# A gated attention and mixture-of-experts layer: twenty held tiles in place of twelve, a shorter gate chain and rows normalized by ScalarE

## The chip, the cores and the metric

The kernel runs on one core of a Trainium2 chip, in float32 throughout. Its time is the device time of one execution in microseconds. "Before" is the median of three runs; the profile is of one further execution.

Engines: PE is TensorE (matrix multiply), DVE is VectorE, ACT is ScalarE, POOL is GpSimd, SP is SyncE, which issues most DMAs. In the trace each engine starts its instructions in the order in which the program puts them, so an instruction that waits holds up all behind it on its engine.

## The reference

Input is `x`, 8 sequences of 512 tokens with 1024 features, and a context of the same shape. Cut to what matters:

```
x = x + tanh(g_xattn) * mlstm(layernorm(x), ctx, ctx, Wi, bi, Wf, bf, ln_scale)
x = x + tanh(g_ffn)   * moe(layernorm(x), router, gate, up, down, shared_gate, shared_up, shared_down)

mlstm(q, k, v):                       # 16 heads of 64
    ig, fg = [q k v] @ Wi + bi, [q k v] @ Wf + bf
    log_f  = log_sigmoid(fg);  cum = cumsum(log_f)
    log_D  = cum[s] - cum[t] + ig[t]  for t <= s, else -inf
    m      = max over t of log_D;  D = exp(log_D - m)
    C      = (q k^T / 8) * D
    h      = (C / (max(|sum C|, exp(-m)) + 1e-6)) @ v
    return per-head layernorm(h) * ln_scale

moe(y):                               # 4096 tokens, 16 experts of width 512, top 2
    shared = (silu(y @ shared_gate) * (y @ shared_up)) @ shared_down      # width 1024, every token
    routed = sum over the two best experts of weight * expert(y)
    return shared + routed
```

## The kernel before

The 4096 tokens are 32 tiles of 128 rows (`NT`), four to a sequence. The work has two stages.

**The attention loop** (`for i in range(1, NT)`, L856) takes one tile per turn and is pipelined by hand: in turn `i` the queries, keys and gates of tile `i + 1` are prepared while tile `i` gets its scores and values, and tile `i - 1` is finished: normalized per head, added to `x`, normalized (`finish_rows`), written out as `y`, transposed (`turn_rows`) and routed (`route_products`, `finish_route`, then `route_group` and `place_group` once per four tiles).

The steps of one tile that the prediction follows are these. `prep_gates` multiplies the partial sums by `sums` into `pg` (L464, one per tile, pinned behind the second half of the scores of the tile before). The 16x128 gate rows then pass between DVE and ACT: `f` (L471, bias L473), `z = min(-f, f)` (L477), its exponential, `u = 1 + z`, its logarithm, a correction of that logarithm (L481 to L489: it multiplies `ln(u)` by `z / (u - 1)`, with a guard for `u = 1`), then two scans, and `nm`, the negated running maximum (L501). `nm` is written to DRAM (L505) and read back broadcast over 128 partitions into `d` (L506). `prep_columns` (L530 and after) transposes the rows into `cols`, and POOL cuts the upper triangle off `d` (L535). `prep_weights` exponentiates `d` on ACT, one head after the other (L577), `scores` multiplies it by the products of queries and keys (L586 on PE, L593 on DVE) in two halves of eight heads; both halves use the two PSUM banks with tag `a`, so the second waits for the DVE product of the first. After the second half comes the next tile's `pg`.

**The shared expert in the loop.** For all tiles but the last 12 (4 x `HELD`), the shared expert is cut into units of work for TensorE: per pair of tiles eight chunks (`chunk`, L248: gate and up for 128 hidden columns, then Silu on ACT and a product on DVE) and four half projections (`project_down`, L265). They lie in a queue, `units`; `fill(share)`, called four times per turn, takes as many as `share` has added up to. The first four turns have a share of 0.75, the later ones of

```
each = (6 * (NT - 4 * HELD) - 1 - 3 * FIRST - RESERVE) / (4 * (NT - 1 - FIRST))
```

which is 99/108 = 0.917 with `HELD = 3`. Eight units (`RESERVE`) are left for the end of the loop. `behind` holds the last instruction of the last unit run, and `pinned` puts an instruction behind it in its engine's order. The chunks' weights are streamed from DRAM again for each pair.

**The experts and the held tiles** (`for e in range(JOBS)`, `JOBS = NE + 2 * HELD`): sixteen jobs for the routed experts, then two jobs per four held tiles, for which half the shared expert's hidden columns are one more "expert" over 512 tokens. All use a seven-product scheme in place of eight block products (`Step`, `down_tiles`), whose sums of blocks DVE and POOL make.

A scheduler orders each engine's instructions from the program's order, dependencies and priorities, so units stand interleaved with the loop's steps. Loads of `x` and `kv` (`load_x`, `load_kv`) and all traffic of the loop go through SP's queue; at the start some loads go through ACT's queue. `row_stats` (L124, L126) makes mean and variance on DVE, `inverse_deviation` the reciprocal deviation on POOL (L114, L117), and `normed` the normalized row on DVE (L426), twice per tile.

Of the kernel before, what the change touches and what calls it, by code (L numbers as in the profile page):

```python
# [18 lines left out]
P = 128  # L19
S = 512  # L20
D = 1024
# [14 lines left out]
HELD = 3  # L36
# [6 lines left out]
def flamingo_layer(  # L43
# [50 lines left out]
    nc.scalar.dma_start(gates_t[:, 0:1], g_xattn.unsqueeze(0).to_broadcast([P, 1]))  # L94
    nc.scalar.dma_start(gates_t[:, 1:2], g_ffn.unsqueeze(0).to_broadcast([P, 1]))
# [210 lines left out]
    with ExitStack() as actx:  # L306
# [50 lines left out]
        nc.scalar.dma_start(lnsc, ln_scale.unsqueeze(0).to_broadcast([P, D]))  # L357
# [21 lines left out]
        nc.scalar.dma_start(acc_d[T : T + P, :], zeros[:, :D])  # L379
# [44 lines left out]
        def normed(row, mean, rstd):  # L424
            o = wk.tile([P, D], F32, tag="row", name="row", bufs=2)
            normed.last = nc.vector.tensor_scalar(o, row, mean, rstd, ALU.subtract, ALU.mult).ins  # L426
            return o

        def prep_norm(i: int):
            q = toks[i]  # L430
            mv = row_stats(sm, q.x)
            rstd = inverse_deviation(sm, mv[:, 1:2], LN_EPS, [P, 1])
            q.xn = normed(q.x, mv[:, 0:1], rstd)
# [25 lines left out]
        def prep_gates(i: int, after=()):  # L459
# [16 lines left out]
            z, u, lnu, eq = (row(n, 1) for n in ("z", "u", "lnu", "eq"))  # L476
# [4 lines left out]
            nc.vector.tensor_scalar(u, u, -1.0, None, ALU.add)  # L481
# [997 lines left out]
```

## Time and profile before

| | |
|---|---|
| runs before | 3212.82 us median of 3 (3210.32 to 3215.99) |
| the profiled execution | 3221.06 us |
| its span, first to last instruction | 3219.3 us |
| mean granted TensorE clock | 0.975 |
| attention loop, to the experts' first product | 1453.1 us |
| experts' jobs, 1453.1 to 2752.4 us | TensorE busy 1296.9 of 1299.3 us |
| the rest of the held jobs, 2752.4 to 3219.3 us | TensorE busy 455.6 of 466.9 us |

TensorE's busy time is a union of modelled matmul spans, so it says where TensorE had work, not that it ran at its peak. A row of a stretch gives its start and end, its length, the busy time of PE, PE's weight loads, DVE, ACT and POOL with the number of instructions, then the granted clock, the share of the DMA engines' time and the GB/s. A row of the timeline gives start, length, engine, line, operation, the tile written and those read, and the shapes; in square brackets the idle time ahead of it and what ended it. TensorE issues each float32 matmul as two instructions, so a half projection of eight matmuls shows as x16.

### The profile page before, as it was taken

How to read it: one execution, taken by the hardware profiler on the slowest of the kernel's cores; microseconds unless marked ns; L12 is line 12 of the kernel's file. 1: busy time of each engine (PE TensorE's matmuls, PEld its weight loads, DVE VectorE, ACT ScalarE, POOL GpSimd, SP SyncE). 2: the span in 40 equal slices, each digit the busy share in tenths (PEclk: the TensorE clock that was granted, in tenths of full speed). 3: DMA queues.
4: the chain of work that ended last, by engine and by line, in shares of the span. 5: the costliest groups of instructions: out<-in, count | busy, mean ns of one | idle time of the engine just before them, and what ended most of it. 6: DMA issues, size and time to landing. Idle time of an engine off the chain costs nothing.

```text
span 3219.3 us, 42324 instructions
## 1 busy us (share of the span) xinstructions
PE 3107.8 (97%) x16127; PEld 2294.8 (71%) x16127; DVE 1798.4 (56%) x3573; ACT 863.7 (27%) x1825; POOL 1295.2 (40%) x993
## 2 busy tenths in 40 slices
PE   6999989999999999999999999999999999999999
PEld 5778777786877867666666666666677777776666
DVE  5655666767667675644444444444454445455554
ACT  3444444443544544311111111111111111100000
POOL 2213232323231323235555555555565544444342
PEclk7889999999999999999999999999999999999999
DMA  6766565666656666553544545444454544645330
GB/s 191 206 210 190 174 181 171 191 187 187 197 170 191 184 188 174 161 198 130 141 121 115 141 134 136 122 119 128 129 142 135 141 129 131 187 163 173 106 130 27
DMA packets 371280, 501.52 MB, mean 156 GB/s; under 512 B 24352, under 2 KB 262480, under 8 KB 366944
## 3 DMA queue, kind: packets, MB, share of 16 engines
q1 hardware_dynamic: 342560, 425.00, 42.1%
q0 software_dynamic: 24752, 72.44, 10.8%
q8 instruction: 130, 2.13, 0.3%
q10 hardware_dynamic: 3760, 1.31, 0.2%
q14 instruction: 78, 0.64, 0.1%
HBM read 394.57 MB, written 114.61 MB: 158 GB/s over the span
## 4 chain that ended last, share of the span: by engine, by line
PE 51%; DVE 3%; issue 0%; DVEq 0%
PE pq L1281 48%; PE ptx L1199 2%; PE pq L1382 1%; DVE hsum L1345 1%; DVE hsum L1346 1%; DVE hT L1303 1%; DVE up L1302 0%; DVE tsum L1230 0%; DVE tsum L1228 0%; DVE tsum L1227 0%; DVE yo L1356 0%; DVE hT L1347 0%; DVE u L1363 0%; DVE u L1362 0%; DVE xT L1202 0%
## 5 line engine op out<-in xcount | busy, mean ns | idle before, releaser
L1281 PE MATMUL pq<-xT,w 128*128 128x256 f32 (+1 forms) x2112 | 513.4, 393 | 8.5 <-DVEq L1262 8.5
L1281 PEld LDWEIGHTS pq<-xT,w 128*128 128x128 f32 x2112 | 401.7, 191 | 101.3 <-issue 13.4
L1281 PE MATMUL pq<-tsum,wsum 128*128 128x256 f32 (+1 forms) x1408 | 349.8, 391 | 0.0
L248 PE MATMUL pgu<-sh_yT,swg 128*128 128x256 f32 (+1 forms) x1280 | 299.2, 384 | 1.3 <-DMA swg<-L_ffn_shared_gate_w_dram 1.3
L1281 PEld LDWEIGHTS pq<-tsum,wsum 128*128 128x128 f32 x1408 | 264.0, 190 | 49.5
L265 PE MATMUL pso<-sh_down,sh_hT 128*128 128x512 f32 x640 | 286.8, 599 | 2.3 <-DVE sh_hT L254 2.3
L248 PE MATMUL pgu<-sh_yT,swu 128*128 128x256 f32 (+1 forms) x1280 | 278.1, 371 | 0.9 <-DMA swu<-n_L_ffn_shared_up_w_dram 0.9
L248 PEld LDWEIGHTS pgu<-sh_yT,swu 128*128 128x128 f32 x1280 | 235.3, 191 | 31.5 <-DMA swu<-n_L_ffn_shared_up_w_dram 1.1
L1305 DVE TENSOR_TENSOR hT<-pq,u 128x256 f32<-128x256 f32 (+1 forms) x176 | 77.2, 439 | 322.4 <-PE pq L1281 318.8
L248 PEld LDWEIGHTS pgu<-sh_yT,swg 128*128 128x128 f32 x1280 | 233.1, 197 | 33.5 <-issue 3.2
L114 POOL TENSOR_SCALAR ve<-bmv 128x1 f32<-128x1 f32 x64 | 15.6, 243 | 580.7 <-DVE bmv L126 578.5
L1246 POOL TENSOR_TENSOR wsum<-w 128x512 f32<-128x512 f32 x88 | 113.6, 1290 | 295.1 <-PE pq L1281 290.8
L265 PEld LDWEIGHTS pso<-sh_down,sh_hT 128*128 128x128 f32 x640 | 119.0, 192 | 136.8 <-issue 132.1
L1302 DVE TENSOR_TENSOR up<-pq,u 128x256 f32<-128x256 f32 (+1 forms) x176 | 77.1, 438 | 223.7 <-PE pq L1281 222.3
L1012 POOL DMA_INDIRECT acc_d<-yo,row_i x64 | 102.1, 1595 | 184.4 <-ACT yo L1374 70.4
L1281 PE MATMUL pq<-wd,hT 128*128 128x512 f32 x352 | 169.6, 597 | 6.9 <-DVE hT L1303 5.4
L1281 PE MATMUL pq<-xT,wsum 128*128 128x256 f32 (+1 forms) x704 | 174.9, 391 | 0.0
L1281 PE MATMUL pq<-tsum,w 128*128 128x256 f32 (+1 forms) x704 | 174.9, 391 | 0.0
L1306 ACT ACTIVATE hT<-hT 128x256 f32<-128x256 f32 (+1 forms) x176 | 75.4, 429 | 339.2 <-DVE hT L1305 339.2
L1281 PE MATMUL pq<-dsum,hT 128*128 128x512 f32 x352 | 165.4, 592 | 0.0
L1281 PE MATMUL pq<-dsum,hsum 128*128 128x512 f32 x352 | 165.4, 592 | 0.0
L1356 DVE TENSOR_TENSOR yo<-pq,u 128x512 f32<-128x512 f32 x176 | 118.9, 686 | 76.9 <-PE pq L1281 56.5
(265 smaller groups left out, 5478.4 us busy)
## 6 DMA issues: line engine op xcount, KB each, us to landing
swg<-L_ffn_shared_gate_w_dram SPq DMA_DIRECT2D x88, 512.0 KB, 5.0
swu<-n_L_ffn_shared_up_w_dram SPq DMA_DIRECT2D x88, 512.0 KB, 5.8
w<-in_L_ffn_gate_w_dram SPq DMA_DIRECT2D x16, 2048.0 KB, 9.8
w<-in_L_ffn_up_w_dram SPq DMA_DIRECT2D x16, 2048.0 KB, 9.9
wd<-in_L_ffn_down_w_dram SPq DMA_DIRECT2D x16, 2048.0 KB, 8.0
d<-nm_d SPq DMA_DIRECT2D x31, 1024.0 KB, 6.2
x_sb<-in_x_dram SPq DMA_DIRECT2D x32, 512.0 KB, 4.9
kv<-in_ctx_dram SPq DMA_DIRECT2D x32, 512.0 KB, 6.0
```

Source lines behind the costliest of these rows:

```text
L248: last = nc.tensor.matmul(pg[:, half, :n], lhsT=w[:, c, :], rhs=st["yT"][:, c, :n], start=(c == 0), stop=(c == NC - 1),)
L265: last = nc.tensor.matmul(po, lhsT=st["hT"][:, k, t * P : (t + 1) * P], rhs=sh_down[:, k, cols], start=(k == 0), stop=(k == 2 * NFC - 1),)
L1012: nc.gpsimd.indirect_dma_start(out=rows, out_offset=bass.IndirectOffsetOnAxis(ap=index, axis=0), in_=row, in_offset=None, compute_op=ALU.add,)
L1199: nc.tensor.transpose(pt[:, c, :], row[:, (half * 4 + c) * P : (half * 4 + c + 1) * P], ident)
L1246: nc.gpsimd.tensor_tensor(s1, a21, a22, ALU.add)
L1281: nc.tensor.matmul(out, lhsT=left[:, c, :], rhs=right[:, c, :], start=(c == 0), stop=(c == chunks - 1))
L1302: nc.vector.tensor_tensor(up, part, other, ALU.add)
L1303: nc.vector.tensor_tensor(out, out, up, ALU.mult)
L1305: nc.vector.tensor_tensor(out, part, other, ALU.add)
L1306: nc.scalar.activation(out, out, AF.Silu)
L1345: nc.vector.tensor_tensor(s1, a21, a22, ALU.add)
L1356: nc.vector.tensor_tensor(rows[t][:, halves[half]], part, other, ALU.add)
```

## The change

`HELD` goes from 3 to 5: the last 20 tiles are held, 12 have units in the loop, there are 26 jobs in place of 22, and `each` becomes 51/108 = 0.472. The other edits: rows are normalized by ACT with a scale and a bias per partition (the bias made by POOL); the gates' logarithm is corrected by subtracting the rounding error `(u - 1) - z` without the division, and `bias_f` is added in ACT's copy; `y` is turned, and its routing products made, one unit and half the values later; the two pinned instructions of routing and columns are now pinned behind the last unit; `kv` has three buffers and is loaded along with `x`; the loads of ACT's queue move to POOL's and, for `wf`, to SP's; and at the start the second tile's norm follows the first tile's gates.

```diff
-HELD = 3
+HELD = 5
...
-    nc.scalar.dma_start(gates_t[:, 0:1], g_xattn.unsqueeze(0).to_broadcast([P, 1]))
-    nc.scalar.dma_start(gates_t[:, 1:2], g_ffn.unsqueeze(0).to_broadcast([P, 1]))
+    nc.gpsimd.dma_start(gates_t[:, 0:1], g_xattn.unsqueeze(0).to_broadcast([P, 1]))
+    nc.gpsimd.dma_start(gates_t[:, 1:2], g_ffn.unsqueeze(0).to_broadcast([P, 1]))
...
-            nc.vector.bn_stats(st[:, k, :], row[:, k * 512 : (k + 1) * 512])
+            row_stats.last = nc.vector.bn_stats(st[:, k, :], row[:, k * 512 : (k + 1) * 512]).ins
...
-            q.kv = wk.tile([P, D], F32, tag="kv", name="kv")
+            q.kv = wk.tile([P, D], F32, tag="kv", name="kv", bufs=3)
...
-        nc.scalar.dma_start(w3[:, :, NH:], wf.rearrange("(c p) h -> p c h", p=P))
+        nc.sync.dma_start(w3[:, :, NH:], wf.rearrange("(c p) h -> p c h", p=P))
...
-        nc.scalar.dma_start(bias_i, bi.unsqueeze(1))
-        nc.scalar.dma_start(bias_f, bf.unsqueeze(1))
+        nc.gpsimd.dma_start(bias_i, bi.unsqueeze(1))
+        nc.gpsimd.dma_start(bias_f, bf.unsqueeze(1))
...
-        nc.scalar.dma_start(lnsc, ln_scale.unsqueeze(0).to_broadcast([P, D]))
+        nc.gpsimd.dma_start(lnsc, ln_scale.unsqueeze(0).to_broadcast([P, D]))
...
-        nc.scalar.dma_start(acc_d[T : T + P, :], zeros[:, :D])
+        nc.gpsimd.dma_start(acc_d[T : T + P, :], zeros[:, :D])
...
-            nc.scalar.dma_start(rw, router_w)
+            nc.gpsimd.dma_start(rw, router_w)
...
-        def normed(row, mean, rstd):
+        def normed(row, mv):
+
+            rstd = inverse_deviation(sm, mv[:, 1:2], LN_EPS, [P, 1])
+            shift = sm.tile([P, 1], F32, tag="shift", name="shift")
+            nc.gpsimd.tensor_scalar(shift, mv[:, 0:1], rstd, -1.0, ALU.mult, ALU.mult)
             o = wk.tile([P, D], F32, tag="row", name="row", bufs=2)
-            normed.last = nc.vector.tensor_scalar(o, row, mean, rstd, ALU.subtract, ALU.mult).ins
+            nc.scalar.activation(o, row, AF.Identity, scale=rstd, bias=shift)
             return o
...
-            nc.scalar.copy(f, pg[32:48, :])
+            nc.scalar.activation(f, pg[32:48, :], AF.Identity, bias=bias_f)
             nc.vector.tensor_scalar(a, pg[0:NH, :], bias_i, None, ALU.add)
-            nc.vector.tensor_scalar(f, f, bias_f, None, ALU.add)
...
             nc.scalar.activation(lnu, u, AF.Ln)
-            nc.vector.tensor_scalar(u, u, -1.0, None, ALU.add)
-            nc.vector.tensor_scalar(eq, u, 0.0, None, ALU.is_equal)
-            nc.vector.tensor_add(u, u, eq)
-            nc.vector.reciprocal(u, u)
-            nc.vector.tensor_mul(u, u, z)
-            nc.vector.tensor_mul(lnu, lnu, u)
-            nc.vector.tensor_mul(eq, eq, z)
-            nc.vector.tensor_add(lnu, lnu, eq)
-            nc.vector.scalar_tensor_tensor(f, f, 0.0, lnu, ALU.min, ALU.subtract)
+            nc.vector.scalar_tensor_tensor(u, u, -1.0, z, ALU.add, ALU.subtract)
+            nc.vector.scalar_tensor_tensor(f, f, 0.0, u, ALU.min, ALU.add)
+            nc.vector.tensor_sub(f, f, lnu)
...
-        def prep_columns(i: int):
+        def prep_columns(i: int, after=()):
             q, last, first = toks[i], i % NS == NS - 1, i % NS == 0
             pc = ps.tile([P, 5, NH], F32, tag="tr", name="pc")
-            nc.tensor.transpose(pc.rearrange("p k h -> p (k h)"), rows3[i % 2], ident[:80, :80])
+            with ExitStack() as order:
+                pinned(order, after)
+                nc.tensor.transpose(pc.rearrange("p k h -> p (k h)"), rows3[i % 2], ident[:80, :80])
...
-        with tc.issue_after(normed.last):
+        with tc.issue_after(row_stats.last):
             prep_gate_weights()
             prep_values(0)
         gate_products(0)
         prep_gates(0)
         prep_columns(0)
-        with tc.issue_after(normed.last):
+        with tc.issue_after(toks[0].gated):
             prep_norm(1)
-        with tc.issue_after(normed.last):
             prep_router()
...
             if i + 2 < NT:
                 load_x(i + 2)
+                load_kv(i + 2)
             fill(share)
             values(i, 0)
             values(i, 1)
             if nxt:
                 prep_values(i + 1)
+            fill(share)
             if back:
                 turn_rows(i - 1)
-            fill(share)
-            if back:
-                route_products(i - 1)
             values(i, 2)
             valued = values(i, 3)
-            if back:
-                whole = finish_route(i - 1, valued)
             head_scale(i)
             if not last:
                 grow(i)
-            if i + 2 < NT:
-                load_kv(i + 2)
+            if back:
+                with tc.issue_after(valued[0]):
+                    route_products(i - 1)
+            fill(share)
+            if back:
+                whole = finish_route(i - 1, behind)
             if nxt:
-                prep_columns(i + 1)
-            fill(share)
+                prep_columns(i + 1, behind)
```

`prep_norm` and `finish_rows` now pass the statistics to `normed`, which calls `inverse_deviation` itself; `toks[i].gated` is the instruction that makes `nm`.

More of the change, by code (lines that the diff above doesn't have):

```diff
@@ L430, in prep_norm @@
             q = toks[i]
-            mv = row_stats(sm, q.x)
-            rstd = inverse_deviation(sm, mv[:, 1:2], LN_EPS, [P, 1])
-            q.xn = normed(q.x, mv[:, 0:1], rstd)
+            q.xn = normed(q.x, row_stats(sm, q.x))
         def prep_values(i: int):
@@ L470, in prep_gates @@
             a, en, w = (rows3[i % 2][32 * k : 32 * k + NH, :] for k in range(3))
-            nc.scalar.copy(f, pg[32:48, :])
+            nc.scalar.activation(f, pg[32:48, :], AF.Identity, bias=bias_f)
             nc.vector.tensor_scalar(a, pg[0:NH, :], bias_i, None, ALU.add)
-            nc.vector.tensor_scalar(f, f, bias_f, None, ALU.add)
-            z, u, lnu, eq = (row(n, 1) for n in ("z", "u", "lnu", "eq"))
+            z, u, lnu = (row(n, 1) for n in ("z", "u", "lnu"))
             nc.vector.scalar_tensor_tensor(z, f, -1.0, f, ALU.mult, ALU.min)
@@ L500, in prep_gates @@
             nm = row("nm", 1)
-            nc.vector.tensor_scalar(nm, q.m, -1.0, None, ALU.mult)
+            q.gated = nc.vector.tensor_scalar(nm, q.m, -1.0, None, ALU.mult).ins
             q.d = wk.tile([P, NH, P], F32, tag="d", name="d")
@@ L679, in finish_rows @@
             nc.sync.dma_start(x1_d[i] if i < NT - 4 * HELD else acc_d[i * P : (i + 1) * P, :], q.x)
-            mv = row_stats(sm, q.x)
-            rstd = inverse_deviation(sm, mv[:, 1:2], LN_EPS, [P, 1])
-            q.y = normed(q.x, mv[:, 0:1], rstd)
+            q.y = normed(q.x, row_stats(sm, q.x))
             nc.sync.dma_start(y_d[i * P : (i + 1) * P, :], q.y)
@@ L845, in flamingo_layer @@
         load_x(2)
+        load_kv(2)
         prep_columns(1)
-        load_kv(2)
         route_products(0)
```

## The prediction
> **What bounds the kernel now.** I read the busy table first, then the slices, then stretches of the two stages, then single instructions. The busy table and the TensorE slices:
>
> ```profile
> PE 3107.8 (97%) x16127; PEld 2294.8 (71%) x16127; DVE 1798.4 (56%) x3573; ACT 863.7 (27%) x1825; POOL 1295.2 (40%) x993
> PE   6999989999999999999999999999999999999999
> ```
>
> The reader is to see one bound, TensorE, in nearly every slice. But it is made of two stages. Up to about 1453 us the attention loop runs, with the shared expert's matmuls strewn between its steps; after that the experts and the held tiles run. `pg` (L464) comes once a tile, so its times cut the loop into tiles: 219.5 us is tile 5's, 1313.4 us tile 31's, 26 tiles in 1093.9 us, 42.07 us each. The stretch, and inside it one single tile (569.0 to 604.9), by busy time:
>
> ```profile
> core 0: us, PE busy (x) PEld busy (x) DVE busy (x) ACT busy (x) POOL busy (x), PEclk, DMA share, GB/s
> 219.50:1313.40 1093.90, 1048.62 (x7198) 816.12 (x7196) 741.85 (x1637) 494.73 (x1104) 298.61 (x258) 0.96 0.62 183
> 569.00:604.90 35.90, 34.25 (x278) 29.45 (x277) 27.33 (x65) 21.19 (x45) 8.15 (x7) 1.00 0.70 203
> ```
>
> Per tile TensorE is busy 40.33 of 42.07 us, DVE 28.5, ACT 19.0, POOL 11.5. What a unit of shared-expert work costs is read off TensorE's timeline: a half projection (L265) from its start to the next instruction, and a chunk (L248, gate and up):
>
> ```profile
> 605.21 7.13 PE L265 MATMUL pso<-sh_down,sh_hT 128*128 128x512 f32 x16
> 612.18 0.39 PE L608 MATMUL pav<-state,eb 128*128 128x130 f32 x2
> ...
> 647.92 3.72 PE L248 MATMUL pgu<-sh_yT,swg 128*128 128x256 f32 x16
> 654.93 0.39 PE L608 MATMUL pav<-state,eb 128*128 128x130 f32 x2
> ```
>
> That is 6.97 and 7.01 us, 6.99 on the mean. A held job, in the chain of waits (start, length), has a fixed period at the end of the kernel:
>
> ```profile
> 2825.98 66.64 PE pq L1281 x262
> 2899.52 66.64 PE pq L1281 x262
> ```
>
> 2899.52 - 2825.98 = 73.54 us a job, with DVE's sums between the two included.
>
> **The change, part by part.** *Eight tiles more are held.* A pair of tiles costs 8 chunks and 4 half projections in the loop, so four pairs take 48 units out: 48 x 6.99 = 335.5 us. By the formula for `each` a tile's share falls from 4 x 0.917 to 4 x 0.472 units, 1.78 fewer, over the 27 tiles from 5 on: 12.43 us each. Added are two quartets of two jobs: 4 x 73.54 = 294.2 us, sure, since that stage has no idle TensorE to take them. If the loop shrinks by exactly the TensorE time removed, a tile takes 42.07 - 12.43 = 29.64 us, and the kernel changes by 294.2 - 335.5 = -41.3 us. All else is whether the loop can do 29.64. The break-even is 42.07 - 294.2/27 = 31.17 us a tile: a margin of 1.5 us.
>
> *DVE.* In the stretch L426 takes 42.3 us, now gone to ACT; the bias and nine instructions of the correction, ten groups (L473, L481 to L489) of 6.9, 5.7, 5.7, 7.2, 24.3, 6.9, 7.9, 6.3, 7.1 and 7.1 us, go, 85.1; three new ones of the same 16x128 kind come at about 7.1 each, 21.3. Fewer evictions: 1.78 units at (8 x 0.41 + 4 x 0.74)/12 = 0.52 us (rows L254, L270) are 0.93 a tile. So 28.5 - 1.63 - 2.45 - 0.93 = 23.5 us a tile, 79% of 29.64: not the bound, but fuller than its 68% now.
>
> *ACT.* Two 128x1024 rows a tile with scale and bias. No such row exists; ACT's 128x512 copy takes 0.587 us and its 128x256 row 0.39, so between 0.59 + 2 x 0.197 = 0.98 and twice 0.587 = 1.17; I take 1.1, since the growing part dominates: 2.2 a tile. The Silu evictions fall by 1.19 x 0.384 = 0.46. So 19.0 + 2.2 - 0.5 = 20.7 us, 70%, at nothing while the loop is TensorE's. *POOL* gets `shift`, 2 x 0.22 to 0.24 us (row L114), and the first DMAs of the start. *Routing a unit later, `kv` with a third buffer and loaded sooner*: the waits that these cover are small, in the stretch 5.4 us for `parts`, 3.1 for `yT`, 6.7 for `kv`, 11.6 for the norm's `row`: at most 26.8 us in all, at least 0 (TensorE's other idle time, 45.3 us, may move to the next late thing). I take 0 as the likeliest and keep 26.8 for the low end. *The DMAs of the start* leave ACT's queue, on which the 0.1 KB load of `bias_i` held the sequencer for 6.42 us; the `wf` load instead stands on SP behind `wi`, and the first gate product needs both. Between -4 us (TensorE's 3.0 us wait for `qT` gone, and what follows) and +5 (the second half of `w3` later by half its 10 us); I take 0. *SP's traffic* per tile: 183 GB/s x 42.07 us = 7.70 MB, less 1.19 chunks of 1.05 MB and 8/27 tiles' 1.57 MB of rows: 6.0 MB, in 29.64 us 201 GB/s; the single tile above ran at 203 with TensorE at 34.25 of 35.9.
>
> *The chain of one tile* is the cover that may fail. These are that tile's steps from `pg` to the next `pg`, across engines:
>
> ```profile
> 577.21 0.21 DVE L481 TENSOR_SCALAR u<-u 16x128 f32<-16x128 f32 x1 [0.39 <-ACT lnu L480]
> 581.93 0.28 DVE L489 SCALAR_TENSOR_TENSOR f<-f,lnu 16x128 f32<-16x128 f32 x1
> 583.57 0.21 DVE L501 TENSOR_SCALAR nm<-m 16x128 f32<-16x128 f32 x1
> 586.32 0.34 SPq L506 DMA_DIRECT2D d<-nm_d  x1
> 592.56 2.01 POOL L535 TENSOR_SCALAR_AFFINE_SELECT d<-d 128x2048 f32<-128x2048 f32 x1
> 596.03 4.79 ACT L577 ACTIVATE d<-d,cols 128x128 f32<-128x128 f32 x16
> 599.79 1.27 DVE L593 SCALAR_TENSOR_TENSOR d<-psc,d 128x512 f32<-128x512 f32 x2
> 603.77 1.16 PE L586 MATMUL psc<-qT,kT 64*128 64x128 f32 x16
> 604.86 0.42 PE L464 MATMUL pg<-parts,sums 128*48 128x128 f32 x2
> ```
>
> `nm` 14.6 us after `pg`, the trip through DRAM and the cut to 594.57, the exponentials, the product, the second scores (which need the score banks that the product empties), `pg`. This cannot be shortened by giving TensorE less to do; it can be by the gates' part. From L481 to the end of L489 are 5.0 us, of which one 0.28 us subtraction remains: 4.7 off, 35.9 - 4.7 = 31.2 us. Between the product's end (601.06) and the scores (603.77) TensorE did a chunk; with fewer units up to 2.7 more go: 28.5 us. So the chain's bounds are 28.5 and 31.2 where 29.64 is asked. In the changed program's order `nm` stands behind DVE's reduction of this tile's values for two tiles in three, a new wait, but TensorE has some 8 to 10 us of work from `pg` to the last value, about what the gates' part now takes. I take the chain as just hidden. If it is not, what is late is the next tile's scores, and with them its gates.
>
> *The clock.* A gap costs twice. TensorE waited 1.61 us for `parts` in the first of these stretches; in the next its clock stood at half:
>
> ```profile
> 1196.00:1204.60 8.60, 6.99 (x59) 6.01 (x58) 5.45 (x15) 3.66 (x9) 0.79 (x2) 1.00 0.47 140
> 1204.60:1208.00 3.40, 3.40 (x10) 2.69 (x9) 2.26 (x12) 0.00 (x0) 1.00 (x1) 0.51 0.62 231
> ```
>
> The stretch's mean clock of 0.96 is 44 us lost, already in the 42.07; I leave it so. The Trainium skill (TensorE: Matmul & The Clock Gate, section "Why this matters for your kernels") asks for no idle gap above about 3 us and would find this 1.61 us gap harmless; the row above says otherwise. By the page, a loop with more but shorter gaps would keep its clock, and my sum could lose those 44 us; by the row it gets more half-speed stretches, and the rule speaks against the change only through gaps that it calls too long.
>
> **The rivals.** *Tile chain decides (slower).* If a tile takes over 31.17 us because the gates' chain, not TensorE, sets it, the held jobs cost more than the loop gives back. At 32.5 us: 294.2 - 27 x 9.57 = +36 us; at 33.5, +63. For it: the single tile above had only 3 units, and its chain ran with 1.5 us to spare (594.57 to 596.03), DVE will be 79% full, and a new order puts `nm` behind TensorE's values. Against: 4.7 us leave exactly this chain. *The stalls go too (faster than forecast).* With the 26.8 us of waits and some half-speed time gone, 28.0 us a tile: 294.2 - 27 x 14.07 = -86 us. For it: the edits name those waits; against: a loop with less filler covers fewer of the others. *More half-speed clock, nothing gained.* One 3.4 us half-speed stretch more in each tile is 1.7 us, x 27 = 46: -41 + 46 = +5, about no change. For it: 10% of the time would be idle where now 4% is; against: the unit matmuls are spread in ones and twos between the late steps. That the change doesn't do what it says I exclude: the counts of units and jobs are fixed in the program.
>
> **How the numbers follow.** The forecast (28.7 to 30.7 us a tile, -66 to -12) gets 0.42, the larger gain 0.20, no change within 0.2% (6 us, about what this kernel's runs can tell) 0.08, the tile chain 0.30. So faster 0.62, same 0.08, slower 0.30. The profiled run has a span of 3219.3 us in 3221.06; the sum is made against it: 3219.3 - 41.3 = 3178. The runs' median is 3212.82, 8.2 below the profiled time, so 3212.8 - 41.3 = 3171.5. The forecast's own range is 3147 to 3201; with the other cases, to -95 (27.6 us a tile) and to +35, it is 3118 to 3248.
>
> **What would show it.** Right: `pg` to `pg` about 29.6 us from tile 8 on, TensorE busy near 26.5 of it, ten held jobs of 73.5 us, `nm` 10 to 12 us after `pg`. Wrong: tiles of over 31 us with TensorE waiting for `d` or the score banks; a clock under 0.93 in the loop; ACT waiting on POOL's `rstd` with the gates' exponentials queued behind; a first `pg` later than 24 us.

## The result, and the profile after

The changed kernel takes 3301.55 us, the median of four runs (3301.09 to 3306.25); the kernel before took 3214.4 (3210.32 to 3219.75) beside it. The ratio is 1.0273, interval 1.0255 to 1.0292: slower by 2.7%, where a gain of 1.3% was forecast. The profiled execution has a span of 3299.3 us, 80.0 more than before.

First the busy table and TensorE's slices of the changed kernel:

```profile
PE 3127.4 (95%) x15967; PEld 2289.6 (69%) x15967; DVE 1806.3 (55%) x3493; ACT 922.8 (28%) x1890; POOL 1469.1 (45%) x1144
PE   6898998988989989999999999999999999999999
```

The loop is now the first fifteen slices, not eighteen, and seven of these show an 8, where before one did. The other twenty-five show a 9. The chain of waits gives the held jobs:

```profile
2538.40 66.64 PE pq L1276 x262
2611.95 66.64 PE pq L1276 x262
```

2611.95 - 2538.40 = 73.55 us a job, as forecast, so four more cost 294.2 us. The experts' first product comes at 1238.5 us, before at 1453.1: the loop gave back 214.6 us, not 335.5. 294.2 - 214.6 = 79.6 is nearly the whole difference of the spans. The loop's middle, from the `pg` of tile 5 to that of tile 31, in the view of stretches (columns as before):

```profile
214.40:1121.10 906.70, 813.76 (x6086) 629.23 (x6084) 608.76 (x1357) 510.53 (x1100) 335.24 (x310) 0.94 0.57 174
```

906.70 / 26 = 34.87 us a tile, where 29.64 was asked and 31.17 is the break-even. What fills a tile can be worked out from TensorE's rows and clock records of this stretch: the time without a matmul; the time lost to half clock (the granted clock was 0.50 in these stretches, so half of the time that TensorE was busy in them); and the rest, which is work at full clock. The forecast leaves the first two as they were.

| us a tile | before | forecast | after |
|---|---|---|---|
| TensorE idle | 1.74 | 1.74 | 3.57 |
| lost to half clock (of 3.02 and 4.07 us at half) | 1.32 | 1.32 | 1.76 |
| work at full clock | 39.01 | 26.58 | 29.54 |
| tile | 42.07 | 29.64 | 34.87 |

Of the 5.23 us that are missing, 1.83 are idle time, 0.44 clock and 2.96 lie inside what counts as work. There, with each matmul counted from the end of the one before and half of it taken off at half clock, units take 14.96 us where 13.19 were due: 2.04 units a tile are left in this stretch, not 1.89 (1.0 us, which the end of the loop gets back: from tile 31's `pg` to the first product it fell from 139.7 to 117.4), and one takes 7.33 us, not 6.99 (0.7 us). Scores take 3.19 us, not 2.23: one matmul instruction is as long as before (0.27 us in the median), but they overlap less. Why units and scores take longer, no run shows.

What TensorE waited for in the stretch (microseconds in all, times, longest):

```profile
PE pt L408 <- ACT row L430: 44.7, 28, 6.6
PE pl L703 <- ACT parts L421: 9.2, 7, 2.0
PE psc L584 <- DVE d L591: 7.6, 6, 1.6
PE pgu L248 <- issue: 4.3, 1, 4.3
```

Before, the norm's row was the largest wait too, but a small one:

```profile
PE pt L408 <- DVE row L426: 11.6, 8, 3.0
```

Now TensorE waits for it 28 times, 44.7 us. ACT's waits in the same stretch:

```profile
ACT row L430 <- POOL shift L428: 142.6, 42, 10.5
...
ACT d L575 <- POOL d L533: 11.3, 6, 4.5
```

ACT stands before the rows, with all behind it on its queue; for the cut `d`, a late step of the prediction's chain, only 6 of 26 tiles' exponentials waited, 11.3 us in all. One of the row's turns in the timeline of the changed kernel:

```profile
684.55 0.97 POOL L783 DMA_INDIRECT table_d<-rowid,slots_i  x1 [0.30 <-issue]
685.60 0.24 POOL L114 TENSOR_SCALAR ve<-bmv 128x1 f32<-128x1 f32 x1
685.92 0.60 POOL L117 TENSOR_TENSOR rstd<-ve,mhalf 128x1 f32<-128x1 f32 x1
686.62 0.90 POOL L428 TENSOR_SCALAR shift<-bmv,rstd 128x1 f32<-128x1 f32 x1
687.55 1.24 ACT L430 ACTIVATE row<-x_sb,shift,rstd 128x1024 f32<-128x1024 f32 x1 [2.86 <-POOL shift L428]
688.85 1.09 PE L408 MATMUL pt<-ident,row 128*128 128x128 f32 x8 [2.44 <-ACT row L430]
```

The first line is the last of eight scatters of the routing table that POOL had ahead of this row: the statistics were there at 682.25 us, and POOL takes them up at 685.60. The path from the statistics to the row has grown: a third POOL step (this `shift` took 0.90 us, the median one 0.27) and 1.24 us on ACT. From the end of the statistics to the end of the row it is 3.53 us on the mean, before 2.26. TensorE stood still for 2.44 us of it.

### The profile page after: what moved, and what is told of

It reads as the page before. It is cut to its first block, busy times and chain, and to the rows that moved or that the text cites. A ratio compares the mean times of both kernels' runs of the same rounds, so it can differ in the third digit from the quotient of the medians.

```text
span 3299.3 us, 42418 instructions
## 1 busy us (share of the span) xinstructions
PE 3127.4 (95%) x15967; PEld 2289.6 (69%) x15967; DVE 1806.3 (55%) x3493; ACT 922.8 (28%) x1890; POOL 1469.1 (45%) x1144
## 3 DMA queue, kind: packets, MB, share of 16 engines
q0 software_dynamic: 25200, 73.55, 10.7%
## 4 chain that ended last, share of the span: by engine, by line
PE 58%; DVE 4%; issue 0%; DVEq 0%
PE pq L1276 55%; PE ptx L1194 2%; DVE hsum L1340 1%; PE pq L1377 1%; DVE hsum L1341 1%; DVE hT L1298 1%; DVE up L1297 0%; DVE tsum L1225 0%; DVE tsum L1222 0%; DVE tsum L1223 0%; DVE hT L1342 0%; DVE yo L1351 0%; DVE u L1358 0%; DVE u L1357 0%; DVE xT L1197 0%
## 5 line engine op out<-in xcount | busy, mean ns | idle before, releaser
L1276 PE MATMUL pq<-xT,w 128*128 128x256 f32 (+1 forms) x2496 | 602.0, 391 | 9.0 <-DVEq L1257 9.0
L1276 PEld LDWEIGHTS pq<-xT,w 128*128 128x128 f32 x2496 | 475.0, 191 | 113.7 <-issue 24.5
L1276 PE MATMUL pq<-tsum,wsum 128*128 128x256 f32 (+1 forms) x1664 | 410.3, 389 | 0.0
L1276 PEld LDWEIGHTS pq<-tsum,wsum 128*128 128x128 f32 x1664 | 312.6, 190 | 56.1
L1330 POOL TENSOR_TENSOR dsum<-wd 128x1024 f32<-128x1024 f32 x52 | 139.4, 2878 | 177.4 <-PE pq L1276 177.4
L248 PE MATMUL pgu<-sh_yT,swg 128*128 128x256 f32 (+1 forms) x768 | 190.5, 385 | 15.0 <-DMA sh_yT<-yT_d 7.7
L265 PE MATMUL pso<-sh_down,sh_hT 128*128 128x512 f32 x384 | 186.4, 618 | 0.0
L248 PE MATMUL pgu<-sh_yT,swu 128*128 128x256 f32 (+1 forms) x768 | 182.2, 374 | 0.0
L1276 PEld LDWEIGHTS pq<-xT,wsum 128*128 128x128 f32 x832 | 158.1, 190 | 30.0
L1276 PEld LDWEIGHTS pq<-tsum,w 128*128 128x128 f32 x832 | 158.1, 190 | 30.0
## 6 DMA issues: line engine op xcount, KB each, us to landing
w<-in_L_ffn_up_w_dram SPq DMA_DIRECT2D x16, 2048.0 KB, 10.1
```

The lines of the kernel that those rows point to most:

```text
L248: last = nc.tensor.matmul(pg[:, half, :n], lhsT=w[:, c, :], rhs=st["yT"][:, c, :n], start=(c == 0), stop=(c == NC - 1),)
L265: last = nc.tensor.matmul(po, lhsT=st["hT"][:, k, t * P : (t + 1) * P], rhs=sh_down[:, k, cols], start=(k == 0), stop=(k == 2 * NFC - 1),)
L1276: nc.tensor.matmul(out, lhsT=left[:, c, :], rhs=right[:, c, :], start=(c == 0), stop=(c == chunks - 1))
L1330: nc.gpsimd.tensor_tensor(out, p, q, ALU.subtract)
```

## The experiments

All runs in one table. A tile is the mean from tile 5's `pg` to tile 31's of one profiled execution, split as above, all in microseconds: "half" is the time at half clock, "work" TensorE's busy time less half of what falls into it; `nm` is its mean end after `pg`. A ratio is taken to runs of the kernel before beside it. In eight experiments the result lay well outside every range that had been expected. Held tiles alone, early routing, 16 held, gates first, `nm` spread by TensorE and the changed kernel with 28 held were slower than any; the kernel before with 28 held, and two idle matmuls, lay between two ranges.

| kernel | held | ratio to before (interval) | tile | idle | half | work | nm |
|---|---|---|---|---|---|---|---|
| before | 12 tiles | 1 | 42.07 | 1.74 | 3.02 | 39.01 | 15.5 |
| after | 20 | 1.0273 (1.0255 to 1.0292) | 34.87 | 3.57 | 4.07 | 29.54 | 14.4 |
| before, held only | 20 | 1.0624 (1.0594 to 1.0654) | 38.63 | 4.43 | 10.11 | 29.86 | 21.1 |
| edits without held | 12 | 1.0066 (1.0041 to 1.0091) | 42.28 | 1.96 | 2.63 | 39.42 | 8.8 |
| after, rows on DVE | 20 | 1.0272 (1.0236 to 1.0309) | 34.73 | 3.33 | 4.07 | 29.69 | 14.6 |
| after, early routing | 20 | 1.0487 (1.0460 to 1.0514) | 36.91 | 4.04 | 8.40 | 29.27 | 14.2 |
| edits, rows on DVE | 12 | 1.0000 (0.9980 to 1.0020) | 42.21 | 1.94 | 2.10 | 39.47 | 9.8 |
| edits, rows and routing as before | 12 | 1.0022 (1.0002 to 1.0042) | 42.43 | 1.84 | 3.54 | 38.98 | 12.3 |
| after, 16 held | 16 | 1.0319 (1.0289 to 1.0348) | 40.36 | 4.07 | 5.65 | 33.94 | 9.6 |
| after, gates first on DVE | 20 | 1.0421 (1.0391 to 1.0450) | 36.96 | 4.87 | 5.51 | 29.76 | 11.0 |
| after, nm spread by TensorE | 20 | 1.0971 (1.0930 to 1.1012) | 41.65 | 3.03 | 14.57 | 31.80 | 8.3 |
| after, no scatters | 20 | 1.0242 (1.0194 to 1.0291) | 34.90 | 3.49 | 4.33 | 29.50 | 14.2 |
| after, 28 held | 28 | 1.1289 (1.1222 to 1.1355) | 36.19 | 8.88 | 25.17 | 17.46 | 16.5 |
| before, 28 held | 28 | 1.1582 (1.1516 to 1.1649) | 39.76 | 11.20 | 30.27 | 17.08 | 22.4 |
| 28 held, 2 idle matmuls | 28 | 1.1106 (1.1065 to 1.1146) | 33.91 | 3.89 | 11.55 | 24.62 | 14.9 |
| 28 held, 4 idle matmuls | 28 | 1.1302 (1.1270 to 1.1334) | 36.13 | 4.88 | 4.99 | 29.52 | 11.1 |
| after, d from old row | 20 | 1.0226 (1.0197 to 1.0255) | 35.04 | 4.22 | 4.07 | 29.07 | 14.4 |
| 28 held, d from old row | 28 | 1.1074 (1.1045 to 1.1103) | 34.27 | 8.23 | 21.42 | 17.77 | 16.8 |
| after, rows not waited for | 20 | 1.0213 (1.0176 to 1.0250) | 34.19 | 3.10 | 3.54 | 29.59 | 14.5 |
| after, both | 20 | 1.0295 (1.0264 to 1.0325) | 35.15 | 4.54 | 6.04 | 28.19 | 11.9 |

### Which part of the change costs

**Held tiles alone**: the kernel before with one line changed.

```diff
-HELD = 3
+HELD = 5
```

> The kernel before with HELD = 5 and nothing else. Theory C (one tile's chain from gates to gates sets the loop once filler is taken out, whatever the other edits do): the chain still has the 4.7 us of the division, so a tile takes 35 to 37 us, 26 of them from the fifth on, and the kernel is at or above the changed one: 3300 to 3350 us. Theory N (the changed kernel is slow because the rows' norm on ACT waits for POOL and holds up ACT's queue and TensorE's transposes): without that edit the loop follows TensorE, about 30 to 31.5 us a tile, 3170 to 3225 us.

3404.86 us, 6.2% slower. TensorE's clock over the loop's middle fell from 0.96 to 0.87, and the score banks became its first wait there:

```profile
PE psc L586 <- DVE d L593: 33.1, 12, 7.7
PE pt L408 <- DVE row L426: 24.5, 15, 5.0
```

**All other edits alone**: the changed kernel with `HELD = 3`.

```diff
-HELD = 5
+HELD = 3
```

> The changed kernel with HELD = 3: all edits but the twenty held tiles. Theory N: the wait on ACT's rows, 45 us of TensorE's idle time in the changed kernel, is there at HELD = 3 too, in part behind filler: 10 to 40 us slower than before, 3225 to 3255 us. Theory C: the edits shorten the chain and do no harm while TensorE has filler: 0 to 25 us faster than before, 3190 to 3213 us.

3226.02 us, 0.7% slower, though `nm` comes 6.7 us earlier than before: with TensorE full, the tile is no shorter for it (42.28 us). So the held tiles cost, and the edits are worth 0.0351 of the ratio (1.0624 less 1.0273), some 113 us, with 20 held tiles, where with 12 they cost 0.7%.

**Rows by DVE again**, at 20 held tiles and at 12:

```diff
-            shift = sm.tile([P, 1], F32, tag="shift", name="shift")
-            nc.gpsimd.tensor_scalar(shift, mv[:, 0:1], rstd, -1.0, ALU.mult, ALU.mult)
...
-            nc.scalar.activation(o, row, AF.Identity, scale=rstd, bias=shift)
+            nc.vector.tensor_scalar(o, row, mv[:, 0:1], rstd, ALU.subtract, ALU.mult)
```

> The changed kernel with the rows normalized by DVE as before, all else as changed. Theory N: TensorE's 45 us of waits for ACT's rows and the half-speed clock behind them mostly go: 40 to 80 us faster than the changed kernel, 3220 to 3260 us. Theory C: within 15 us of the changed kernel, 3285 to 3315 us, since another step of the chain is late in its place.

> The changed kernel with the rows normalized by DVE and HELD = 3. At twelve held tiles the edits cost 0.7%. If ACT's rows (39 us of TensorE's waits in that run) are the cause, it falls to 3185 to 3212 us; if the waits only change their name, as at HELD = 5, it stays at 3215 to 3235 us.

At 20 held tiles nothing changes (1.0272 beside 1.0273): the path of the row is shorter again, and TensorE waits 41.1 us for it in the stretch instead of 44.7. At 12 held tiles DVE's rows are better by 0.7% (1.0000 beside 1.0066, intervals apart). So the longer row path is a cost of the change, but not the one that decides.

**Turning, routing and columns as before**, in the changed kernel:

```diff
+            if back:
+                turn_rows(i - 1)
             fill(share)
             if back:
-                turn_rows(i - 1)
+                route_products(i - 1)
             values(i, 2)
             valued = values(i, 3)
+            if back:
+                whole = finish_route(i - 1, valued)
...
-            if back:
-                with tc.issue_after(valued[0]):
-                    route_products(i - 1)
+            if nxt:
+                prep_columns(i + 1)
             fill(share)
-            if back:
-                whole = finish_route(i - 1, behind)
-            if nxt:
-                prep_columns(i + 1, behind)
```

> The changed kernel with the rows turned, routed and put in columns where the kernel before does it (and no pin behind the last unit). Theory N: within 15 us of the changed kernel, 3285 to 3315 us. Theory R (the later place of turning and routing puts its DMAs and the score transposes between the gates and their round trip through DRAM, which takes 5.2 us from nm to the read's issue in place of 3.0): 20 to 60 us faster, 3240 to 3280 us.

3362.06 us: moving them later is worth 0.0214 of the ratio, some 69 of the 113 us. TensorE waited 60.7 us for the row, and stood at half clock for 8.4 us a tile. What Theory R gives for the trip is not the mean: from `nm` to the read's issue the changed kernel takes 3.2 us (tiles 5 to 30) and the kernel before 2.8.

**What remains at 12 held tiles**: the shorter gates, `kv` and the start's loads, with rows on DVE and routing as before (the diffs of `HELD = 3`, of the rows and of the routing above, together).

> HELD = 3 with the short gates, the third buffer of kv and the moved DMAs, but the rows normalized by DVE and turned and routed where they were. If TensorE's work sets the tile at twelve held tiles, the edits are worth only the start: within 0.4% of before, 3200 to 3226 us. If the shorter gates free time there too: 3170 to 3200 us.

1.0022: 0.2% slower, with an interval that only just leaves out no change. The edits that were to shorten the loop's chains shorten nothing while units cover them.

**Sixteen held tiles** (`HELD = 4`):

```diff
-HELD = 5
+HELD = 4
```

> The changed kernel with HELD = 4: 2.78 units a tile. If TensorE's work alone sets a tile, it takes 42.3 - 6.2 = 36.1 us and the kernel 3200 to 3212 us, better than with HELD = 3. If the chain of about 35 us is already felt, as queues that miss each other, the tile takes 37 to 38.5 us and the kernel 3230 to 3265 us.

3316.48 us. The price does not grow evenly with the held tiles. From 12 to 16 of them, with all the edits, 6.2 us of units leave a tile and it gets 1.9 us shorter (42.28 to 40.36); from 16 to 20 it gets 5.5 us shorter. So the loop falls behind TensorE's work already at 40 us a tile, and TensorE waits 64.1 us for rows there. `nm` is early (9.6), so `nm` isn't what this loop is late by.

### Which wait sets the tile

**Gates first**: on DVE the values, turned rows, head scale and state of a tile are pinned behind the next tile's `nm`.

```diff
+            first_gates = ExitStack()
             if nxt:
+                first_gates.enter_context(tc.issue_after(toks[i + 1].gated))
                 prep_values(i + 1)
+            first_gates.close()
             fill(share)
+            first_gates = ExitStack()
+            if nxt:
+                first_gates.enter_context(tc.issue_after(toks[i + 1].gated))
             if back:
                 turn_rows(i - 1)
...
+            first_gates.close()
```

> The changed kernel (HELD = 5) with DVE's instructions of the next tile's values, of the turned rows, of the head scale and of the state put behind the next tile's nm in DVE's order; no other edit. Theory Q (the gates are fast, but nm stands on DVE behind about 3.2 us of work of these kinds a tile, and the time that they wait for TensorE): nm comes 10 to 12 us after pg in place of 14.4 and a tile takes 31 to 32.7 us in place of 34.9: 3195 to 3245 us. Rival (the chain closes over another late step, the turned rows or the head scale): nm earlier, but the tile still 33.5 to 36 us: 3270 to 3330 us.

`nm` came 3.4 us earlier, and the tile grew by 2.1 us: now the rows and the state were late, in TensorE's waits of the loop's middle:

```profile
PE pt L408 <- ACT row L430: 53.8, 26, 7.2
PE pst L635 <- ACT sq L618: 14.3, 9, 2.5
```

**Without the trip through DRAM**: `nm` is spread over the partitions by TensorE, as for tile 0.

```diff
-                nc.sync.dma_start(nm_d[i], nm)
-                nc.sync.dma_start(q.d, nm_d[i].unsqueeze(0).to_broadcast([P, NH, P]))
...
-            if i == 0:
+            if True:
```

> The changed kernel (HELD = 5) with nm spread over the partitions by TensorE for every tile, as it is for the first (16 small matmuls, about 2 us a tile, and the triangle cut after the exponential), in place of the trip through DRAM. Theory C: the chain loses the trip and the cut, 12 us from nm to the exponentials, and gets about 4: the tile falls to what TensorE needs with 2 us more, 30 to 32.5 us: 3180 to 3240 us. Rival (the loop isn't bound by this chain but by DVE's and ACT's queues): the tile stays at 34 to 36 us: 3280 to 3330 us.

3522.93 us. The 16 matmuls into `pm` (32 instructions) take 4.2 us a tile and share the units' bank `g`, and TensorE stands at half clock for 14.6 us a tile. This costs more than the trip, so it says little about it.

**Without the table's scatters** after the first group:

```diff
             for k in range(n):
                 for a in range(2):
+                    if first > 0:
+                        continue
                     nc.gpsimd.indirect_dma_start(
```

> The changed kernel (HELD = 5) without the table's 48 scatters in the loop after the first group of four tiles (so the experts gather token 0 for most slots, in the same number of jobs). They hold POOL for 10 us in every fourth tile, in front of the reciprocal deviations that ACT's rows wait for. If POOL's queue is what makes the rows late: tiles 10, 14, 18, 22, 26 and 30 fall from 37.3 to about 33 us, and the kernel by 25 to 60 us to 3240 to 3275 us. If it is one late step among several: under 15 us faster.

The tile stays at 34.90 us. POOL's scatters stand in the way of some rows (as the one ahead of 685.60 us in the timeline above), but TensorE's time for rows only falls from 44.7 to 34.7 us, and other waits take it.

**d from the old row**: the cut's data come from the row of the tile before, at 20 held tiles and at 28.

```diff
-                nc.sync.dma_start(q.d, nm_d[i].unsqueeze(0).to_broadcast([P, NH, P]))
+                nc.sync.dma_start(q.d, nm_d[max(i - 1, 1)].unsqueeze(0).to_broadcast([P, NH, P]))
```

> The changed kernel, with d read from the row of the tile before in place of its own (so the weights of the attention are other numbers, and the output differs; the work is the same). The chain from nm through DRAM to the cut no longer holds d: its read can go as soon as the buffer is free. Theory C (this chain sets the tile): the exponentials come 6 us or more earlier after pg (29.0 now), the tile falls to 29.6 to 31.5, the kernel by 27 x 3.4 to 27 x 5.2 = 92 to 140 us, to 3160 to 3210. Theory S or K (no one chain: when this wait goes, rows, values or the score banks are late, and the clock is as it was): the tile stays at 33.5 to 35, the kernel within 35 us of 3302.

> The same edit of d's read (the output differs) on the loop almost without units (HELD = 7, 36.19 us a tile). Theory C: the tile falls by 6 us or more, to 30 or less, and the kernel from 3635 to under 3475. Theory K: TensorE at half clock still has 27 us of work in it, and the tile falls by 1 to 4 us. Theory S: within 1 us.

That the trip really left the chain is seen in the group of `d`'s 31 reads: count, duration in ns (least, median, most), first and last start. In the changed kernel, where tile 31's `pg` is at 1121.1 us, and then in the one with the old row and 20 held tiles, where it is at 1122.0:

```profile
L502 SPq DMA_DIRECT2D d<-nm_d x31: 319/338/1378, 72.5 to 1137.3; - x31
```

```profile
L502 SPq DMA_DIRECT2D d<-nm_d x31: 319/339/911, 72.2 to 1108.0; - x31
```

The last read starts 16.2 us after that `pg` in the one and 14.0 us ahead of it in the other. On the mean of tiles 5 to 30 the reads now start 16.0 us before the tile's `pg`, not 17.6 after it, and the cut ends 6.0 us before it, not 26.5 after. The columns, the other thing that the exponentials need from the gates, are there 20.7 us after `pg`. Yet the exponentials start 29.2 us after it (29.0 in the changed kernel), and the tile is 35.04 us: they are pinned behind the copies of the next tile's turned queries on ACT, which end at 28.5 us, and these follow TensorE, which now waits 62.1 us for rows:

```profile
PE pt L408 <- ACT row L430: 62.1, 31, 6.4
```

With 28 held tiles the same edit is worth 1.9 us. As the sole limit, the chain over `nm`, DRAM and the cut is refuted at 20 held tiles.

**Rows not waited for**, alone and together with the edit above:

```diff
-            q.turned = transposed(q.qT, lambda c: q.xn[:, c * P : (c + 1) * P], [nc.scalar.copy] * 2)
+            q.turned = transposed(q.qT, lambda c: q.x[:, c * P : (c + 1) * P], [nc.scalar.copy] * 2)
...
-                yT, lambda c: q.y[:, c * P : (c + 1) * P], [nc.scalar.copy, nc.vector.tensor_copy]
+                yT, lambda c: toks[min(i + 1, NT - 1)].x[:, c * P : (c + 1) * P], [nc.scalar.copy, nc.vector.tensor_copy]
```

> The changed kernel, but TensorE turns rows that lie there long before: the queries come from x as loaded in place of its normalized row, and the router's and shared expert's rows from the x of the tile after in place of y (the output differs). The normalized rows are still made and y still written, so each engine's work is as before; only TensorE's wait for statistics, POOL's deviation and ACT's row is gone (44.6 us of its 90.4 us of waits over 0.25 us in tiles 5 to 31). If that chain of rows alone sets the tile: 34.87 falls by 1.7 to 3.5 us to 31.4 to 33.2, the kernel by 45 to 95 to 3207 to 3257. If two chains stand at one level (this one and nm's trip through DRAM, whose removal alone left 35.04): each hides the other, the tile stays at 33.8 to 35.2. If TensorE's order and the engines' queues in general set it: 33.8 to 35.2 too.

> Both freed: d read from the row of the tile before, and TensorE's turned rows from x as above (the output differs). If the two chains stand at one level and only together set the tile: 29.6 to 31.5 us, kernel 3155 to 3210. If not (what waits next is the values' evictions, the score banks, the columns, with a clock at half in some 4 us a tile): 32.5 to 35, kernel 3235 to 3305.

With the row not waited for, its 44.7 us of waits are gone, and the stretch is only 17.8 us shorter (0.68 a tile). In their place, in TensorE's waits of the first of the two:

```profile
PE pst L635 <- POOL state L627: 17.4, 7, 3.9
PE psc L584 <- DVE d L591: 13.9, 10, 3.3
PE psc L584 <- DVE state L644: 9.3, 6, 3.4
PE pgu L248 <- DMA sh_yT<-yT_d: 8.7, 3, 3.3
```

With both edits the tile is 35.15. The four corners of the table, 34.87, 35.04, 34.19 and 35.15, speak against two chains that hide each other. (Each edit lets the scheduler order the engines anew, so a few tenths between such kernels are no finding.)

### The loop without units

**28 held tiles**, with the edits, and (from the kernel before) without:

```diff
-HELD = 5
+HELD = 7
```

> The changed kernel with HELD = 7: only four tiles have units, and from the fifth tile on a turn has 0.03 of a unit at each call, so that the loop runs almost without filler. It measures the loop's floor. Theory C (one tile's chain sets the loop): a tile takes 28.5 to 32 us though TensorE has only 13 to 14 us of work in it, so that filler in excess of some 15 us a tile is what costs. Theory M (the units and the chain delay each other in TensorE's fixed order; the chain alone is short): 20 to 26 us a tile.

> The kernel before with HELD = 7, for its loop's floor. Theory C with the division worth 4.7 us and the other edits little: 4 to 6 us a tile above the same run of the changed kernel. If the division is not on the path of an empty loop: within 2 us of it.

A loop with next to no units takes 36.19 us a tile, longer than the 34.87 with two units in it. Its stretch:

```profile
216.20:1157.10 940.90, 710.13 (x4938) 602.67 (x4936) 590.03 (x1313) 445.31 (x1024) 334.33 (x310) 0.65 0.38 122
```

The clock is 0.65. TensorE stands at half in 25.2 of 36.2 us, so that work which takes 17.5 us at full clock keeps it busy for 710.13 / 26 = 27.3. The edits are worth 3.6 us a tile here.

**Idle matmuls**: pure TensorE work that waits for nothing, two or four 128x512 matmuls at each place of units.

```diff
+    def spin(n: int):
+        po = ps.tile([P, 512], F32, tag="o", name="spun")
+        for k in range(n):
+            last = nc.tensor.matmul(
+                po, lhsT=sh_down[:, k, :P], rhs=sh_down[:, k, :512], start=(k == 0), stop=(k == n - 1)
+            )
+        behind[:] = [last.ins]
...
             fill(share)
+            if i > FIRST:
+                spin(2)
```

> Fourteen jobs' worth of held tiles (HELD = 7) as in the run before it, which left the loop almost without units (36.19 us a tile, of which TensorE idle 8.88, and 25.17 at half clock), but with two 128x512 matmuls at each of the four places of the loop where units go. They read constant weights, wait for no data, and nobody reads their result: pure TensorE work of 4 x 2 x 0.87 = 7.0 us a tile. Theory K (the loop with little filler is slow because TensorE's clock stands at half): the added work holds the clock, the tile gets SHORTER, 29 to 33 us, the loop's clock rises from 0.65 to over 0.85, the kernel falls from 3635 to 3460 to 3550 us. Theory C (the chain of one tile over nm and the trip through DRAM sets it, whatever TensorE's clock): the work goes into the idle time, the tile stays within 1 us of 36.2 and the kernel within 27 us of 3635. Theory S (TensorE's order: each late step holds up all behind it, so added work adds): 38 to 43 us a tile, kernel 3690 to 3820.

> The same with four such matmuls at each place: 13.9 us of TensorE work a tile, about what the changed kernel's units are (14.96 us a tile in its trace), but without their loads, evictions and waits. Theory K: with the clock held the tile is TensorE's work of 17.5 + 13.9 = 31.4 us and some 1 to 2 us of waits, 32 to 34 us: shorter than the changed kernel's 34.87 by what the units themselves cost on other engines and queues. Theory C: 34.5 to 36.5, as in the changed kernel. Theory S: 37 or more.

The stretch with two matmuls, then the one with four:

```profile
214.20:1095.80 881.60, 780.57 (x5346) 570.39 (x5344) 583.53 (x1312) 438.88 (x1025) 328.67 (x310) 0.83 0.40 130
```

```profile
210.80:1150.10 939.30, 812.45 (x5637) 535.44 (x5635) 584.85 (x1309) 428.32 (x1013) 319.80 (x310) 0.93 0.38 120
```

7.2 us of useless TensorE work a tile make the tile 2.3 us shorter: the clock goes from 0.65 to 0.83, which brings what is lost at half clock from 9.9 to 5.4 us, and TensorE's idle time goes from 8.9 to 3.9 us. So the clock has a real part in the slow loop, though the gain is smaller than Theory K expected (29 to 33 us). The added matmuls also move the instructions that are pinned behind the last unit, so the clock may not be all of it. The next 6.9 us make the tile 2.2 us longer, with the clock at 0.93, and TensorE waits for rows:

```profile
PE pt L416 <- ACT row L438: 100.6, 35, 9.0
```

The tile of 36.13 us lies in the range of Theory C, against which the runs with `d` from the old row speak. It has about as much filler as the changed kernel and none of the units' own loads and evictions, so the loop is slow without these too.

## Why the prediction was wrong

**The step that failed** is the one on which the sum stands: "If the loop shrinks by exactly the TensorE time removed, a tile takes 42.07 - 12.43 = 29.64 us", with its covers ("All else is whether the loop can do 29.64", "I take the chain as just hidden", the gain from waits taken as 0, the clock "I leave it so"). That sum holds idle time, clock and the price of a unit fixed while filler goes. The runs showed in its place 34.87 us a tile: 1.83 us more idle time, 0.44 more lost to the clock and 2.96 more inside the work. The loop falls behind TensorE's work already with 16 held tiles (40.36 us where 36.1 was due), and it doesn't get under some 34 us: of all fifteen kernels with 20 or 28 held tiles none had a tile under 33.9, whatever filled it. The break-even of 31.17, worked out in the prediction, was right, and these tiles are past it.

**Readings in the prediction that don't fit its own lines.** The "other idle time, 45.3 us" is TensorE's whole idle time in the stretch (1093.90 - 1048.62), the 26.8 us included. "TensorE busy near 26.5" of 29.6, and with it "10% of the time would be idle", doesn't follow from the sum: 40.33 - 12.43 leaves 27.9 us busy, and it was 813.76 / 26 = 31.3. And the range, which ends at +35, leaves out the +63 that the prediction's own rival gives at 33.5 us a tile.

**Units and jobs.** A job measured 73.55 us, as taken. A unit costs 6.99 us in the full loop; the 48 units taken out brought 214.6 us, 4.47 each, and those left take 7.33.

**Gates and the chain of one tile.** "4.7 off" was forecast for the chain, with `nm` 10 to 12 us after `pg`. With 12 held tiles it came even at 8.8; with 20 at 14.4, 1.1 less than before: between `pg` and `nm` DVE then does 12.4 us of work, where it is 7.0 with 12. The centring of the next values (L443, 1.06 us) and the heads' variance (L657, 0.97) come into it, which are not there with 12. The second is the "new wait" that the prediction saw and took as hidden. But the failure isn't there: an earlier `nm` made the tile no shorter, and without the trip the tile of 20 held stayed. The bounds 28.5 and 31.2 were the bounds of a chain that doesn't set the tile.

**The rival "tile chain decides"** (0.30) has the right side and neither mechanism nor size: +36 at 32.5 us, +63 at 33.5; it is +80 on the span, at 34.87.

**The waits.** The prediction took the gain from the waits that the edits name (26.8 us) as 0, and put no loss into the sum. The wait for rows alone went from 11.6 to 44.7 us, and TensorE's idle time rose by 1.83 x 26 = 48 us. One sign that the prediction listed for being wrong is there: ACT waiting for POOL's part of the norm, 142.6 us.

**The clock.** "Left so" cost 0.44 us a tile, 11 us, and mean clock 0.94 stays above the 0.93 that was named. Its rival ("more half-speed clock", +5) is real, but a small part here; it is large in the kernels with less cover (10.1 us a tile at half with held tiles alone, 25.2 with 28 held). The stretches at half clock in the loop's middle, 9 before and 15 after, all last whole multiples of 3.41 us. With the time cut into windows of 3.41 us so that the stretches begin and end with a window, the last window ahead of a stretch was at least 46% without a matmul in 22 of the 24, and of the other 508 windows at full clock only 2 were. The prediction's 1.61 us gap lies in such a window whole (47% of it), so that row was the right guide. With held tiles alone it is so for 14 of 23 stretches only, so idle time in one window isn't all of it. The Trainium skill (TensorE: Matmul & The Clock Gate, section "Why this matters for your kernels") asks only for no gap above about 3 us; ahead of 10 of the changed kernel's 15 stretches the longest gap in 8 us was 1.4 to 2.9 us, which speaks against that bound.

**DVE, ACT, SP.** DVE was forecast at 23.5 us a tile and is 608.76 / 26 = 23.4. ACT at 20.7, and is 19.6, though its row takes 1.24 us and not 1.1 (above the upper bound of 1.17). SP's 6.0 MB a tile: 174 GB/s x 34.87 us = 6.07. No engine is a bound by its sum. The start: the first `pg` at 21.4 us, 2.6 later, inside -4 to +5, and tile 5's `pg` is 5.1 us earlier.

**What stays open**: which order of the queues would let the loop go faster. Shown is that each of the known late steps (rows, the DRAM trip, scatters) can go with at most 0.7 us a tile gained at 20 held tiles, while other names come into TensorE's waits. One path was not taken away by any run: the exponentials' pin behind the next tile's turned queries. With `d` from the old row these are there 28.5 us after `pg`, the exponentials run from 29.2 to 34.0, and the next `pg` follows at 35.0: the traces close the tile there, over TensorE's order up to the queries and ACT's exponentials. Whether the tile falls without that pin, no run shows. That it is the in-order queues of five engines, each waiting on another in turn, is what is left over, and is argued, not shown by itself. None of the versions is faster than the kernel before; with 12 held tiles and rows on DVE the edits equal it.

## What to carry to other kernels

Work that stands between the steps of a pipelined loop isn't only cost: it covers waits, and it holds TensorE's clock. Taking it out gives back its full time only while the loop has nothing else to wait for; before counting on that, take nearly all of it out once, and read the tile that is left (36.19 us here, where 31.17 was needed), and the tile with a part of it out (16 held tiles brought 1.9 of 6.2 us). And when one wait is removed and the time stays, look at the list of waits, not at the one that went: here the edits that took a wait away changed the names in it and hardly the tile.

## What the hardware showed unexpectedly

Adding 7.2 us of matmuls that nobody needs to each tile made the tile 2.3 us shorter, with the granted clock rising from 0.65 to 0.83. ACT's 128x1024 row with scale and bias from pointers took 1.24 us (1.224 to 1.242), more than twice its 128x512 copy of 0.587; the Trainium skill (ScalarE: Activation LUTs, section "What ACT_TABLE_LOAD costs") gives 186 ns plus 0.833 ns an element plus 93 ns for each pointer, an estimate of 1.225 us, which agrees. Of POOL's 64 `shift` instructions of one column, the median took 0.27 us and the longest 1.25.
